# A graph attention layer with residual and layer norm: the last blocks put in another order, and a branch's transfers on another queue

## The chip, the cores and the metric

The kernel runs on one core of one Trainium2 chip. The core has five engines that run their own instruction streams: TensorE (PE; its weight loads are shown as PEld), VectorE (DVE), ScalarE (ACT), GpSimd (POOL) and SyncE (SP), which here only issues transfers. Sixteen DMA engines move data between the memory (HBM) and the on-chip memory (SBUF); TensorE writes to PSUM, which VectorE and ScalarE read and GpSimd doesn't. The metric is the device time of one execution in microseconds, as the median of several runs.

## What is computed

```python
def _L0_gnn_ref(h, adj_mat, W, a):          # 4 heads, 512 hidden
    ht = (h @ W).reshape(N, 4, 512).transpose(1, 0, 2)
    src = einsum('hnd,hd->hn', ht, a[:, :512, 0])
    dst = einsum('hnd,hd->hn', ht, a[:, 512:, 0])
    e = leaky_relu(src[:, :, None] + dst[:, None, :], 0.01) + adj_mat[None]
    att = softmax(e, axis=-1)
    return einsum('hij,hjd->hid', att, ht).mean(axis=0)

x = layernorm(x + _L0_gnn_ref(x, adj, W, a), axis=-1)      # eps 1e-5
```

`x` is 4096 x 512 and `adj` 4096 x 4096, both float32 (64 MB of `adj`). The entries of `adj` go up to 1e9 and are added to the scores before the softmax. Where the largest entry of a row leads the second largest by more than the scores can differ, the softmax is 1 at that column and 0 elsewhere, and the row's attention is one row of `x` times the mean of the four heads' `W`.

## The kernel before

`leading_rows` assumes that every row has such a leader, computes the output from it, and then tests whether it was true. `general` computes the whole layer the long way; it stands behind a branch (lines 61 to 63) on the number of rows that fail. With these inputs no row fails and the branch isn't entered. Its instructions are still part of the program, and at the place where the two ways meet each engine brings its semaphores to the values that they would have after the branch.

There are NB = 32 blocks of 128 rows. A loop over t = 0 to 31 is a software pipeline that is written out by hand; the order in the text is the order on each engine. For a block `ib`:

- `load_adj` (L118, SyncE) loads 2 MB of `adj`, five blocks ahead; the last four blocks come in two or four pieces. `load_x` (L121) loads rows of `x` into `hold`, which keeps all 32 blocks and becomes the output.
- `segment_maxima` (L163, VectorE) takes the maximum of each 32 columns; `find_segment` (L168 to L182) finds the segment of the largest one (`at`), and on GpSimd computes its address (`row`), fetches these 32 numbers with an indirect DMA (`lead`) and computes `start`.
- two steps later `find_column` takes the second largest in the segment (`find_inner`), finds the position, computes the column on GpSimd (`col`, L200), and `gather_rows` fetches that row of `x` as `y` (L186, indirect DMA). The last block uses `find_column_in_row` instead: VectorE searches the whole row of 4096 (L206).
- `turn` (L213, L215): four transposes on TensorE, and a copy to SBUF on ScalarE (`yt`). `products` (L228): four products with the mean of the heads' weights, summed in PSUM (`o`). `residual` (L221) adds the block's `x` to the same sum by a product with the identity; `residual_in_halves` (L266) does so for the last block, whose product is made in two halves (L270).
- blocks 0 to 23: `stats` (two ScalarE passes), `rstd` (GpSimd) and `finish` (ScalarE, L261) normalise. `row_norm` (L235) sums the squares of `x` for the test.

BEHIND = 24 and LATE = 28. Blocks 24 to 27 get their `x` late: `put_by` parks the products in SBUF and `add_x` (L244) adds `x` afterwards. Blocks 27 to 31 use `moments` (bn_stats on VectorE, square root on ScalarE, L287), `factor` (L290, L292) and `normalise` (VectorE, L297).

What follows the loop (L463 to L525) is the tail, again in hand-written order: the stores of blocks 0 to 23 (L313), the rest of blocks 24 to 31, the bound and test (`bound`, `test`, `count`, `report`) and the last six stores. All loads and stores of this part are issued by SyncE, in order, on eight semaphores in turn; a transfer waits until the one eight places ahead of it has landed. A store that isn't ready holds up those behind it. GpSimd issues its gathers itself.

In `general` the transfers are issued by GpSimd (L555, L557, L592, L632, L643).

Of the kernel before, what the change touches and what calls it, by code (L numbers as in the profile page):

```python
# [20 lines left out]
P = 128  # L21
# [45 lines left out]
def leading_rows(ctx, tc, x, adj, W, a, out, ident, v, n_bad, any_bad):  # L67
# [100 lines left out]
    def find_segment(ib):  # L168
        seg = seg_of.pop(ib)
        nc.vector.max(out=top[:, ib, :], in_=seg)  # L170
        at = small.tile([P, 8], U32, name="at")
        nc.vector.max_index(at, top[:, ib, :], seg)  # L172
        row = small.tile([P, 1], U32, name="row")
        nc.gpsimd.tensor_tensor(row, at[:, 0:1], first[:, ib : ib + 1], op=OP.add)  # L174
        lead = lead_pool.tile([P, E], F32, name="lead")
        nc.gpsimd.indirect_dma_start(  # L176
            out=lead, out_offset=None, in_=adj_segs,
            in_offset=bass.IndirectOffsetOnAxis(ap=row[:, :1], axis=0),
        )
        start = at_of[ib] = small.tile([P, 1], U32, name="start")  # L180
        nc.gpsimd.tensor_tensor(start, at[:, 0:1], width, op=OP.mult)  # L181
        lead_of[ib] = lead  # L182

    def gather_rows(ib, col):
        y = y_t[ib] = y_pool.tile([P, D], F32, name="y")
# [73 lines left out]
    def finish(ib):  # L259
        i = slice(ib, ib + 1)  # L260
        nc.scalar.activation(hold[:, ib, :], o_ps.pop(ib), AF.Identity, bias=nm[:, i], scale=sd[:, i])  # L261

    def residual_in_halves(ib):
        o_ps[ib] = [psum.tile([P, D // 2], F32, name="o") for _ in range(2)]
        for k, o in enumerate(o_ps[ib]):
            nc.tensor.matmul(o, ident, hold[:, ib, ts(k, D // 2)], start=True, stop=False)  # L266
# [22 lines left out]
    def factor(ib, shift=False):  # L289
        nc.vector.reciprocal(rt[ib], rt[ib])  # L290
        if shift:
            nc.vector.scalar_tensor_tensor(  # L292
                nm[:, ib : ib + 1], mean_var[ib][:, 0:1], -1.0, rt[ib], op0=OP.mult, op1=OP.mult
            )

    def normalise(ib, o, columns=slice(0, D)):
# [107 lines left out]
    vectors = [(kb, h) for kb in range(KB) for h in range(H)]  # L404
    vectors_at = {t: 2 if t < 3 else 1 for t in range(1, 15)}
    COLUMN, PROJECT, STATS, FINISH = 2, 3, 4, 6

    for t in range(NB):
        if t == NB // 2:
            tc.mark_branch_hint_location("general", engines=HINTED)  # L410
        if t in x_at:
            load_x(*x_at[t])
        if t + AHEAD == NB - 1:
            load_x(LATE, Q)
        load_adj(t + AHEAD)
# [12 lines left out]
        if t < 2:  # L428
            mean_of_heads(t)
        elif t == 2:  # L430
            mean_of_heads(2)
            mean_of_heads(3)
        if t == 0:
            turn_a()
        turned = [(*vectors[0], turn_w(*vectors.pop(0))) for _ in range(vectors_at.get(t, 0))]
        if t == 16:
            head_norms()
        ib = t - PROJECT
        if t == NB - 1:
            for late in range(LATE, NB):  # L440
                row_norm(late)
            residual(LATE)
            residual(LATE + 1)
        if ib >= 0:
            turn(ib)
            if ib > BEHIND:
                products(ib - 1, KB - 1, KB)
            if ib < BEHIND:
                residual(ib)
        for some in turned:  # L450
            head_vector(*some)
        if ib >= 0:
            products(ib, 0, KB if ib < BEHIND else KB - 1)
        if t >= BEHIND + STATS:
            put_by(t - STATS)
        elif t >= STATS:
            stats(t - STATS)
            row_norm(t - STATS)
        if pair:
            finish(t - FINISH)  # L460
            finish(t - FINISH + 1)

    for ib in range(BEHIND, LATE):  # L463
        row_norm(ib)
    for ib in range(0, 2 * Q, Q):
        store(nc.sync, ib, Q)
    for ib in range(2 * Q, BEHIND, 2):
        store(nc.sync, ib, 2)
    find_column(NB - 2)
    add_x(nc.gpsimd, BEHIND)  # L470
    add_x(nc.gpsimd, BEHIND + 1)
    find_column_in_row(NB - 1)
    add_x(nc.gpsimd, BEHIND + 2)
    products(LATE, KB - 1, KB)
    residual_in_halves(NB - 1)
    turn(NB - 3)
    products(NB - 3, 0, KB - 1)
    moments(LATE)
    for ib in range(BEHIND, NB):
        find_inner(ib)  # L480
    bound(0)
    products(NB - 3, KB - 1, KB)
    stats(BEHIND)
    factor(LATE)
    normalise(LATE, o_ps.pop(LATE))
    bound(1)
    turn(NB - 2)
    bound(2)
    add_x(nc.vector, LATE - 1)
    stats(BEHIND + 1)  # L490
    moments(LATE - 1)
    products(NB - 2, 0, 2)
    bound(3)
    test()
    pg = count()
    products(NB - 2, 2, KB - 1)
    stats(BEHIND + 2)
    rstd(slice(BEHIND, BEHIND + 2))
    rstd(slice(BEHIND + 2, BEHIND + 3))
    moments(NB - 3)  # L500
    report(pg)
    turn(NB - 1)
    factor(LATE - 1, shift=True)
    factor(NB - 3)
    normalise(NB - 3, o_ps.pop(NB - 3))
    finish(BEHIND)
    finish(BEHIND + 1)
    products(NB - 2, KB - 1, KB)
    products_of_half(NB - 1, 0)
    products_of_half(NB - 1, 1)  # L510
    nc.vector.tensor_add(hold[:, NB - 2, :], o_ps[NB - 2], hold[:, NB - 2, :])
    o_ps[NB - 2] = hold[:, NB - 2, :]
    moments(NB - 2)
    stats_of_half(NB - 1, 0)
    factor(NB - 2)
    normalise(NB - 2, o_ps.pop(NB - 2))
    finish(BEHIND + 2)
    finish(BEHIND + 3)
    stats_of_half(NB - 1, 1)
    moments(NB - 1)  # L520
    factor(NB - 1, shift=True)
    finish_in_halves(NB - 1)
    for ib, n in ((NB - 4, 1), (NB - 3, 1), (BEHIND, 2), (NB - 2, 1), (BEHIND + 2, 2)):
        store(nc.sync, ib, n)
    store(nc.sync, NB - 1, 1)  # L525

# [2 lines left out]
def general(ctx, tc, x, adj, W, out, ident, v, n_bad):  # L529
# [20 lines left out]
    with ExitStack() as pre:  # L550
# [1 line left out]
        two = pre.enter_context(tc.tile_pool(name="two", bufs=2))  # L552
        pps = pre.enter_context(tc.tile_pool(name="pps", bufs=2, space=bass.MemoryType.PSUM))
        for g in range(NCH):
            nc.gpsimd.dma_start(x_sb[:, ts(g, Q), :], x_blocks[:, ts(g, Q), :])  # L555
        for kb in range(KB):
            nc.gpsimd.dma_start(w_sb[:, kb, :], w_blocks[:, kb, :])  # L557
        for g in range(NCH):
            xT = two.tile([P, KB, C], F32, name="xT")
            for q in range(Q):  # L560
# [26 lines left out]
    def block(ib):  # L587
# [1 line left out]
        nc.vector.tensor_copy(src_i, src[:, ds(ib, 1), :].rearrange("p o h -> p (o h)"))  # L589
        held = psum.tile([P, D], F32, name="o_ps", bufs=1)  # L590
        adj_t = score.tile([P, N], F32, name="adj_g")
        nc.gpsimd.dma_start(adj_t, adj[ds(ib, P, NB), :])  # L592
        for h in range(H):
            s = score.tile([P, N], F32, name="s")
            nc.scalar.activation(s, dst_b[:, h, :], AF.Identity, bias=src_i[:, h : h + 1])
# [33 lines left out]
                    start=(h == 0 and kb == 0), stop=(h == H - 1 and kb == KB - 1),  # L629
                )  # L630
        r = turned.tile([P, D], F32, name="y_g")
        nc.gpsimd.dma_start(r, x[ds(ib, P, NB), :])  # L632
        nc.vector.tensor_add(r, r, held)
        st = stat.tile([P, nc.vector.BN_STATS_DIM], F32, name="st_g")
        nc.vector.bn_stats(st, r)
# [4 lines left out]
        nc.scalar.activation(sd, sd, AF.Sqrt)  # L640
        nc.vector.reciprocal(sd, sd)
        nc.vector.tensor_scalar(r, r, mv[:, 0:1], sd, op0=OP.subtract, op1=OP.mult)
        nc.gpsimd.dma_start(out[ds(ib, P, NB), :], r)  # L643

    with tc.For_i(0, NB, 1) as ib:
        of_block = stat.tile([1, 1], I32, name="of_block", bufs=1)
# [32 lines left out]
```

## Time and profile before

| | us |
|---|---|
| runs: median, lowest, highest (3 runs) | 235.95, 235.95, 236.46 |
| the profiled execution | 236.21 |
| its span | 234.6 |
| VectorE busy / TensorE busy | 188.4 / 195.2 |
| ScalarE busy / GpSimd busy | 111.6 / 101.2 |
| moved by the DMA engines | 97.21 MB, 414 GB/s over the span |

Times inside the profile count from the start of its span. The page gives the busy share of each engine in 40 equal slices, the chain of work that ended last, and groups of instructions with their mean duration. Other answers of the trace list instructions in order of time, what an engine waited for, and busy times by stretches. A wait is put down to what ended last before it. The first groups of the page are these (line, engine, operation, output and inputs, shapes, count, busy us and mean ns, idle us before and what ended it):

```profile
L163 DVE TENSOR_REDUCE seg<-adj_t 128x64 f32<-128x2048 f32 (+1 forms) x68 | 146.0, 2149 | 32.7 <-DMA adj_t<-in_adj_dram 32.3
L228 PE MATMUL o<-w_sum,yt 128*128 128x512 f32 x248 | 115.1, 605 | 1.7 <-ACT yt L215 1.7
```

A product counts as two matmuls there, and its 605 ns overlap with the next one: TensorE takes a new product every 0.86 us.

### The profile page before, as it was taken

How to read it: one execution, taken by the hardware profiler on the slowest of the kernel's cores; microseconds unless marked ns; L12 is line 12 of the kernel's file. 1: busy time of each engine (PE TensorE's matmuls, PEld its weight loads, DVE VectorE, ACT ScalarE, POOL GpSimd, SP SyncE). 2: the span in 40 equal slices, each digit the busy share in tenths (PEclk: the TensorE clock that was granted, in tenths of full speed). 3: DMA queues.
4: the chain of work that ended last, by engine and by line, in shares of the span. 5: the costliest groups of instructions: out<-in, count | busy, mean ns of one | idle time of the engine just before them, and what ended most of it. 6: DMA issues, size and time to landing. Idle time of an engine off the chain costs nothing.

```text
span 234.6 us, 2498 instructions
## 1 busy us (share of the span) xinstructions
PE 195.2 (83%) x683; PEld 101.4 (43%) x683; DVE 188.4 (80%) x302; ACT 111.6 (48%) x267; POOL 101.2 (43%) x215
## 2 busy tenths in 40 slices
PE   0188929999999999999979879797998968698990
PEld 0034514756565655555534333242443423244460
DVE  1736875589869995999589989998799999989672
ACT  2012011255474747474758354646464645166582
POOL 1012232414527462646353645464365464549130
PEclk9999977999999999999999999999799999999998
DMA  6999999999999999999999999999999999999985
GB/s 226 439 428 426 443 425 430 415 440 412 440 420 426 424 437 434 425 424 428 427 432 433 425 433 422 432 418 429 425 432 418 422 425 427 411 425 419 417 355 210
DMA packets 13697, 97.21 MB, mean 414 GB/s; under 512 B 2152, under 2 KB 2664, under 8 KB 7792
## 3 DMA queue, kind: packets, MB, share of 16 engines
q1 hardware_dynamic: 10080, 88.08, 88.9%
q0 software_dynamic: 3584, 8.92, 9.6%
q8 instruction: 6, 0.10, 0.2%
q14 instruction: 11, 0.09, 0.1%
q10 hardware_dynamic: 16, 0.02, 0.0%
HBM read 88.62 MB, written 8.39 MB: 414 GB/s over the span
## 4 chain that ended last, share of the span: by engine, by line
DMA 45%; POOL 17%; issue 15%; PE 10%; DVE 9%; ACT 1%; POOLq 0%; SPq 0%; DVEq 0%
DMA adj_t<-in_adj_dram 42%; DVE seg L163 8%; PE o L228 7%; POOL lead L176 6%; POOL y L186 5%; DMA y<-in_x_dram,col 3%; POOL sd L256 2%; PE o L270 2%; POOL start L181 1%; POOL row L174 1%; POOL col L200 1%; PE tp L213 1%; PE o L221 1%; ACT yt L215 1%; POOL sd L255 1%
## 5 line engine op out<-in xcount | busy, mean ns | idle before, releaser
L163 DVE TENSOR_REDUCE seg<-adj_t 128x64 f32<-128x2048 f32 (+1 forms) x68 | 146.0, 2149 | 32.7 <-DMA adj_t<-in_adj_dram 32.3
L228 PE MATMUL o<-w_sum,yt 128*128 128x512 f32 x248 | 115.1, 605 | 1.7 <-ACT yt L215 1.7
L228 PEld LDWEIGHTS o<-w_sum,yt 128*128 128x128 f32 x248 | 44.5, 191 | 54.8 <-issue 42.3
L215 ACT COPY yt<-tp 128x512 f32<-128x512 f32 x32 | 18.8, 588 | 44.3 <-PE tp L213 44.3
L176 POOL DMA_INDIRECT lead<-in_adj_dram,row x32 | 32.3, 1010 | 15.5 <-POOL row L174 15.0
L186 POOL DMA_INDIRECT y<-in_x_dram,col x32 | 30.9, 965 | 15.4 <-POOL col L200 15.2
L318 PE MATMUL o<-hold,ident 128*128 128x512 f32 x32 | 18.9, 745 | 17.5 <-DMA hold<-in_L_gnn_W_dram 17.5
L213 PE MATMUL tp<-ident,y 128*128 128x128 f32 x128 | 20.0, 280 | 12.6 <-DMA y<-in_x_dram,col 12.6
L221 PE MATMUL o<-hold,ident 128*128 128x512 f32 x52 | 27.3, 611 | 0.0
L213 PEld LDWEIGHTS tp<-ident,y 128*128 128x128 f32 x128 | 14.9, 143 | 25.4 <-issue 25.0
L174 POOL TENSOR_TENSOR row<-at,first 128x1 uint32<-128x1 uint32 x32 | 6.1, 190 | 42.0 <-DVE at L172 42.0
L336 ACT COPY wt<-tp 128x512 f32<-128x512 f32 x16 | 9.2, 587 | 31.4 <-PE tp L334 31.4
L200 POOL TENSOR_TENSOR col<-start,within 128x1 uint32<-128x1 uint32 x31 | 5.9, 190 | 40.1 <-DVE within L198 40.1
L235 ACT ACTIVATE sq<-hold 128x512 f32<-128x512 f32 x32 | 19.8, 619 | 0.0
L342 PEld LDWEIGHTS pv<-at_d,wt 128*128 128x128 f32 x128 | 16.3, 191 | 6.8 <-ACT wt L336 4.0
L318 PEld LDWEIGHTS o<-hold,ident 128*128 128x128 f32 x32 | 7.4, 243 | 26.7 <-POOL row L174 11.0
L319 ACT ACTIVATE w_sum<-o 128x512 f32<-128x512 f32 x4 | 2.4, 598 | 33.9 <-PE o L318 33.9
L261 ACT ACTIVATE hold<-o,nm,sd 128x512 f32<-128x512 f32 x24 | 17.2, 771 | 0.0
L252 ACT ACTIVATE sq<-o,nm 128x512 f32<-128x512 f32 x24 | 16.5, 688 | 0.8
L342 PE MATMUL pv<-at_d,wt 128*128 128x2 f32 x128 | 15.3, 244 | 0.6 <-ACT wt L336 0.6
L250 ACT ACTIVATE sq<-o 128x512 f32<-128x512 f32 x24 | 14.6, 609 | 0.0
L334 PEld LDWEIGHTS tp<-ident,hold 128*128 128x128 f32 x64 | 7.9, 142 | 6.9 <-issue 6.9
(85 smaller groups left out, 139.8 us busy)
## 6 DMA issues: line engine op xcount, KB each, us to landing
adj_t<-in_adj_dram SPq DMA_DIRECT2D x27, 2048.0 KB, 31.3
hold<-in_x_dram SPq DMA_DIRECT2D x7, 1024.0 KB, 33.2
adj_t<-in_adj_dram SPq DMA_DIRECT2D x6, 1024.0 KB, 25.7
out_dram<-hold SPq DMA_DIRECT2D x10, 512.0 KB, 15.2
adj_t<-in_adj_dram SPq DMA_DIRECT2D x8, 512.0 KB
hold<-in_L_gnn_W_dram SPq DMA_DIRECT2D x4, 1024.0 KB
out_dram<-hold SPq DMA_DIRECT2D x2, 1024.0 KB
hold<-in_x_dram SPq DMA_DIRECT2D x2, 512.0 KB, 14.1
```

The source lines that it names most:

```text
L163: nc.vector.tensor_reduce(seg_of[ib][:, ts(k, S // n)], adj_t[ib][:, ts(k, N // n)].rearrange("p (s e) -> p s e", e=E), axis=AX.X, op=OP.max,)
L176: nc.gpsimd.indirect_dma_start(out=lead, out_offset=None, in_=adj_segs, in_offset=bass.IndirectOffsetOnAxis(ap=row[:, :1], axis=0),)
L186: nc.gpsimd.indirect_dma_start(out=y, out_offset=None, in_=x, in_offset=bass.IndirectOffsetOnAxis(ap=col[:, :1], axis=0),)
L213: nc.tensor.transpose(tp[:, kb, :], y[:, ts(kb, P)], ident)
L215: nc.scalar.copy(yt, tp)
L221: nc.tensor.matmul(o_ps[ib], ident, hold[:, ib, :], start=start, stop=False)
L228: nc.tensor.matmul(o_ps[ib], yt_of[ib][:, kb, :], w_sum[:, kb, :], start=(start and kb == 0), stop=(kb == KB - 1),)
L235: nc.scalar.activation(sq, hold[:, ib, :], AF.Square, accum_out=xx[:, ib : ib + 1])
L252: nc.scalar.activation(sq, o, AF.Square, bias=nm[:, i], accum_out=sd[:, i])
L261: nc.scalar.activation(hold[:, ib, :], o_ps.pop(ib), AF.Identity, bias=nm[:, i], scale=sd[:, i])
L318: nc.tensor.matmul(o, ident, hold[:, w_at + kb * H + h, :], start=(h == 0), stop=(h == H - 1))
L342: nc.tensor.matmul(pv[:, kb, h : 2 * H : H], wt[:, k, :], at_d[:, k, h : 2 * H : H], start=(k == 0), stop=(k == KB - 1),)
```

## The change

Five things are changed.

1. The transfers of `general` are issued by SyncE instead of GpSimd.
2. `find_segment` is split: its GpSimd part is now `fetch_segment`, which follows at once for all blocks but the last. For block 31 it comes in the tail, behind the gather of block 30 and the add of block 24, and without `start`, which isn't used there.
3. The residual of block 29 leaves TensorE: `add_residual` adds it on VectorE when the product is done, as was done for block 30. The halves' residual of block 31, the turns of 29 and 30 and the last products of 28 and 29 change places. The add of block 27 goes from VectorE to GpSimd.
4. Blocks 24 to 26 are finished on GpSimd (`finish_on_chip`) and block 27 on ScalarE earlier than before. The test's count and report come later.
5. The stores of blocks 0 to 23 and of 24 to 30 are issued in another order, in the same sizes. `factor` uses another VectorE operation for the same product.

```diff
     def find_segment(ib):
...
+        if ib < NB - 1:
+            fetch_segment(ib)
+
+    def fetch_segment(ib):
+        at = at_of.pop(ib)
         row = small.tile([P, 1], U32, name="row")
...
         lead_of[ib] = lead
+        if ib < NB - 1:
+            start = at_of[ib] = small.tile([P, 1], U32, name="start")
+            nc.gpsimd.tensor_tensor(start, at[:, 0:1], width, op=OP.mult)
...
+    def finish_on_chip(ib):
+        i, h = slice(ib, ib + 1), hold[:, ib, :]
+        o_ps.pop(ib)
+        nc.gpsimd.tensor_scalar(h, h, sd[:, i], nm[:, i], op0=OP.mult, op1=OP.add)
+
+    def add_residual(ib):
+        nc.vector.tensor_add(hold[:, ib, :], o_ps[ib], hold[:, ib, :])
+        o_ps[ib] = hold[:, ib, :]
...
-            nc.vector.scalar_tensor_tensor(
-                nm[:, ib : ib + 1], mean_var[ib][:, 0:1], -1.0, rt[ib], op0=OP.mult, op1=OP.mult
+            nc.vector.tensor_scalar(
+                nm[:, ib : ib + 1], mean_var[ib][:, 0:1], rt[ib], -1.0, op0=OP.mult, op1=OP.mult
             )
...
+    HELD = ((8, 2), (10, 2), (0, Q), (12, 2), (14, 2), (Q, Q), (16, 2), (18, 2), (20, 2), (22, 2))
...
             residual(LATE)
-            residual(LATE + 1)
...
-    for ib in range(0, 2 * Q, Q):
-        store(nc.sync, ib, Q)
-    for ib in range(2 * Q, BEHIND, 2):
-        store(nc.sync, ib, 2)
+    for ib, n in HELD:
+        store(nc.sync, ib, n)
     find_column(NB - 2)
     add_x(nc.gpsimd, BEHIND)
-    add_x(nc.gpsimd, BEHIND + 1)
+    fetch_segment(NB - 1)
     find_column_in_row(NB - 1)
-    add_x(nc.gpsimd, BEHIND + 2)
+    for ib in (BEHIND + 1, LATE - 1, BEHIND + 2):
+        add_x(nc.gpsimd, ib)
+    turn(NB - 3)
     products(LATE, KB - 1, KB)
+    products(NB - 3, 0, KB - 1)
+    stats(BEHIND)
+    moments(LATE)
+    bound(0)
     residual_in_halves(NB - 1)
-    turn(NB - 3)
-    products(NB - 3, 0, KB - 1)
-    moments(LATE)
-    for ib in range(BEHIND, NB):
+    for ib in range(BEHIND, NB - 1):
         find_inner(ib)
-    bound(0)
-    products(NB - 3, KB - 1, KB)
-    stats(BEHIND)
+    bound(1)
     factor(LATE)
     normalise(LATE, o_ps.pop(LATE))
-    bound(1)
     turn(NB - 2)
+    products(NB - 3, KB - 1, KB)
     bound(2)
-    add_x(nc.vector, LATE - 1)
     stats(BEHIND + 1)
     moments(LATE - 1)
-    products(NB - 2, 0, 2)
+    find_inner(NB - 1)
     bound(3)
     test()
-    pg = count()
-    products(NB - 2, 2, KB - 1)
+    products(NB - 2, 0, KB - 1)
     stats(BEHIND + 2)
     rstd(slice(BEHIND, BEHIND + 2))
+    finish_on_chip(BEHIND)
+    finish_on_chip(BEHIND + 1)
     rstd(slice(BEHIND + 2, BEHIND + 3))
+    finish_on_chip(BEHIND + 2)
+    add_residual(NB - 3)
+    turn(NB - 1)
     moments(NB - 3)
-    report(pg)
-    turn(NB - 1)
     factor(LATE - 1, shift=True)
+    finish(LATE - 1)
     factor(NB - 3)
     normalise(NB - 3, o_ps.pop(NB - 3))
-    finish(BEHIND)
-    finish(BEHIND + 1)
     products(NB - 2, KB - 1, KB)
     products_of_half(NB - 1, 0)
+    pg = count()
     products_of_half(NB - 1, 1)
-    nc.vector.tensor_add(hold[:, NB - 2, :], o_ps[NB - 2], hold[:, NB - 2, :])
-    o_ps[NB - 2] = hold[:, NB - 2, :]
+    add_residual(NB - 2)
     moments(NB - 2)
     stats_of_half(NB - 1, 0)
     factor(NB - 2)
     normalise(NB - 2, o_ps.pop(NB - 2))
-    finish(BEHIND + 2)
-    finish(BEHIND + 3)
+    report(pg)
     stats_of_half(NB - 1, 1)
     moments(NB - 1)
     factor(NB - 1, shift=True)
     finish_in_halves(NB - 1)
-    for ib, n in ((NB - 4, 1), (NB - 3, 1), (BEHIND, 2), (NB - 2, 1), (BEHIND + 2, 2)):
+    for ib, n in ((LATE, 1), (BEHIND, 2), (NB - 3, 1), (BEHIND + 2, 2), (NB - 2, 1)):
         store(nc.sync, ib, n)
     store(nc.sync, NB - 1, 1)
...
-            nc.gpsimd.dma_start(x_sb[:, ts(g, Q), :], x_blocks[:, ts(g, Q), :])
+            nc.sync.dma_start(x_sb[:, ts(g, Q), :], x_blocks[:, ts(g, Q), :])
...
-            nc.gpsimd.dma_start(w_sb[:, kb, :], w_blocks[:, kb, :])
+            nc.sync.dma_start(w_sb[:, kb, :], w_blocks[:, kb, :])
...
-        nc.gpsimd.dma_start(adj_t, adj[ds(ib, P, NB), :])
+        nc.sync.dma_start(adj_t, adj[ds(ib, P, NB), :])
...
-        nc.gpsimd.dma_start(r, x[ds(ib, P, NB), :])
+        nc.sync.dma_start(r, x[ds(ib, P, NB), :])
...
-        nc.gpsimd.dma_start(out[ds(ib, P, NB), :], r)
+        nc.sync.dma_start(out[ds(ib, P, NB), :], r)
```

More of the change, by code (lines that the diff above doesn't have):

```diff
@@ L170, in find_segment @@
         nc.vector.max(out=top[:, ib, :], in_=seg)
-        at = small.tile([P, 8], U32, name="at")
+        at = at_of[ib] = small.tile([P, 8], U32, name="at")
         nc.vector.max_index(at, top[:, ib, :], seg)
+        if ib < NB - 1:
+            fetch_segment(ib)
+    def fetch_segment(ib):
+        at = at_of.pop(ib)
         row = small.tile([P, 1], U32, name="row")
@@ L179, in find_segment @@
         )
-        start = at_of[ib] = small.tile([P, 1], U32, name="start")
-        nc.gpsimd.tensor_tensor(start, at[:, 0:1], width, op=OP.mult)
         lead_of[ib] = lead
+        if ib < NB - 1:
+            start = at_of[ib] = small.tile([P, 1], U32, name="start")
+            nc.gpsimd.tensor_tensor(start, at[:, 0:1], width, op=OP.mult)
     def gather_rows(ib, col):
```

## The prediction

> **What bounds the kernel now.** I read the page first (span, slices, chain), then the busy time by stretches of the tail, then the chain of waits from 203 us on, and at last the instructions of the lines that open and close the program.
>
> ```profile
> span 234.6 us, 2498 instructions
> ...
> PE   0188929999999999999979879797998968698990
> DMA  6999999999999999999999999999999999999985
> GB/s 226 439 428 426 443 425 430 415 440 412 440 420 426 424 437 434 425 424 428 427 432 433 425 433 422 432 418 429 425 432 418 422 425 427 411 425 419 417 355 210
> ```
>
> Up to slice 38 the DMA engines are full: 97.21 MB at some 425 GB/s. The change moves the same bytes, so all that it can win lies at the start, in the last 10 us, and in what comes after the last store.
>
> ```profile
> 220.00:225.00 5.00, 4.63 (x20) 2.42 (x19) 4.04 (x20) 3.95 (x12) 1.67 (x5) 1.00 1.03 415
> 225.00:230.00 5.00, 4.23 (x18) 2.96 (x16) 3.74 (x9) 3.60 (x7) 0.37 (x2) 1.00 0.78 304
> 230.00:234.60 4.60, 0.00 (x0) 0.00 (x0) 0.78 (x3) 0.83 (x2) 0.00 (x0) 0.84 0.49 192
> ```
>
> These are stretch, length, busy us of PE, PEld, DVE, ACT and POOL, clock, DMA share, GB/s: from 225 us the DMA has holes, because the last stores are not ready. What they wait for is in the chain of waits (start, us, what):
>
> ```profile
> 207.78 1.72 PE o L221 x4
> 209.49 0.44 PE tp L213 x4
> ...
> 214.31 0.86 PE o L266 x4
> 215.17 0.45 PE tp L213 x4
> ...
> 215.64 0.59 ACT yt L215
> ...
> 220.57 0.59 ACT yt L215
> ...
> 225.69 3.55 PE o L270 x16
> ...
> 229.27 0.44 DVE halves_st L304
> ...
> 230.69 0.56 ACT hold L310
> ```
>
> TensorE is the chain from 203.58 to 229.24, with two holes of 0.6 us while ScalarE copies a turned block. Two residuals stand in it (1.72), and the halves' residual of block 31 (0.86) comes where there is no hole. From the last product to the end of ACT L310 it takes 2.01 us; the last store is issued at 231.29 and its semaphore is full at 233.60 (2.31). The program's own end and start, by line (ns shortest/median/longest, first and last start):
>
> ```profile
> L62 POOLq INC_SWDGE_SEM  x1: 1476/1476/1476, 226.7 to 226.7; - x1
> ```
> ```profile
> L674 SPq EVENT_SEMAPHORE  x14: 17/28/28, 232.8 to 234.5; - x14
> ...
> L674 POOLq DRAIN  x3: 40/103/5306, 228.2 to 234.3; - x3
> ```
> ```profile
> L665 POOLq MOVE  x4: 29/29/35, 0.2 to 0.4; - x4
> ```
>
> GpSimd balances its DMA semaphores in the branch not taken (L62, 1.48 us) and then drains for 5.31 us, from 228.23 to 233.54, 0.2 us before SyncE reaches the closing barrier at 233.74. So GpSimd's end is nearly the bound today and would be, were it to get there later. SyncE's twelve closing waits run from 232.83 at 0.064 us each, so that all but the last are over when the store lands.
>
> **What the skill says.** "GPSIMD Engine Reference", 3.1, gives 769 ns measured for a one-input loop over 512 elements and about twice VectorE's time for two inputs; the trace has 1.28 us for the two-input add (L244) against 0.67 us on VectorE, which agrees, and no one-input GpSimd operation of this size. "VectorE: DVE Perf Modes", Why PSUM operands drop a tier, says that a PSUM source loses the faster mode: L297 takes 0.81 us from PSUM and 0.55 from SBUF here. "DMA: Bandwidth & Descriptors", Anatomy of one DMA, puts a fixed cost near 2 us on a transfer, mostly the receipt of the last byte; the last store's 2.31 us for 256 KB agrees.
>
> **The change, part by part.**
>
> Start. The four GpSimd MOVEs at 0.21 to 0.42 us belong to the general path's transfers and go to SyncE, which now waits for GpSimd at the opening barrier. GpSimd's memsets and drain move up 4 x 0.06 = 0.24 us, and the first load with them: -0.24 (bounds 0 to -0.3).
>
> TensorE. From 207.78: one residual 0.86, turn 0.44, last product of 27 0.86, three of 28 2.57, so 212.6. The turn of 29 now comes before the last product of 28, and its gather (issued 206.05) lands at 212.90 by the trace's semaphores: start 213.05. Turn, last of 28, three of 29 end at 216.9: the copy of 29 hides behind 28's product. Transpose of the bound 0.11, halves' residual 0.86: 217.9. The gather of 30 is issued behind `col` alone, at 211.2 instead of 212.00; with its 6.45 us it lands at 217.6, so there is no wait. Turn 0.44, last of 29 0.86, 0.11, three of 30 2.57: 222.0. The gather of 31 stands behind one add instead of two, but behind the moved lead fetch: issue 215.1 instead of 215.65 (VectorE's index ends at 214.84), 7.09 us, landed 222.2. Turn 222.35, product, two halves of 1.78, count 0.11: end 227.4 instead of 229.24.
>
> VectorE. It loses the add of 27 and gets the add of block 29's residual (0.72, paid for by L297 from SBUF, 0.57 for 0.81); the test comes earlier than it is needed. Block 29's root waits on ScalarE behind the copy of 31 (223.6), so normalising 29 ends at 224.7. Then, on VectorE alone: add 0.72, statistics 0.82, half statistics 0.43, reciprocal 0.18, normalise 0.57, report 0.50, in all 3.2: it reaches the last half's statistics at 228.0, not at TensorE's 227.5. Before: 229.27. Gain 1.3; without the report, which earlier stood at 223.4, it would be 1.7. The range is 0.9 (gather latencies of 7.3 and 7.5) to 1.7 (6.4 both).
>
> ScalarE loses three finishes (0.72 each) and is not late. GpSimd: adds of 25, 27, 26 end at 220.0, roots of 24 and 25 1.3, two finishes, root of 26 1.1, one finish. One finish on GpSimd is not in the trace. Bounds: 0.44 us (512 elements at the page's port bound of 1.03 cycles at 1.2 GHz, an estimate) and 2.7 us (twice the two-input row). I take 0.8 (the page's 769 ns): done at 225.6; at 1.25 it is 227.0. The store of 26 and 27 waits for that one, and behind it on SyncE stand the stores of 30 and 31; at up to 2 us it is in time.
>
> Landing. With 1.3 + 0.24, the last store is issued at 229.75 and could land at 232.05. But one of the sixteen DMA engines lags: the store of 28 has fifteen parts by 227.42 and the last at 228.46, and from there this engine has nearly no pause. Its own times are 0.6 us for 256 KB (230.81 to 231.41) and 1.21 for 512 KB (to 232.62). From 228.46 - 0.24: 1.2 + 0.6 + 1.2 + 0.6 + 0.6 gives 232.4 for the last store. Bounds: 232.05 without the lag (231.75 if the latency falls to 2.0, as for its other parts), 233.0 if the 0.55 that the store of 24 and 25 took beyond 1.21 (1.76, an instruction fetch beside it) comes again. I take 232.4: -1.2 against 233.60.
>
> Close. The general path's transfers on SyncE make it balance its eight hardware DMA semaphores in the branch not taken, each a wait for all earlier transfers. The last of these waits for the last store; only then come a branch and the twelve closing waits. Before, the landing was followed by the drain after 0.09 us; now by 0.09 + 0.03 + 12 x 0.064 = 0.88: +0.79 (bounds 0.6 and 1.0). This is new on the path. GpSimd's 1.48 + 5.31 us go; that wins nothing itself (0.2 us of slack), but without it the finishes and the late report, which ends near 228, would have cost about 3 us. Behind the closing waits nothing else is queued.
>
> The new order of the held stores moves no bytes and no start of the queue (199 us); eight stay in flight, at least 4 MB, some 9 us of work: 0, with bounds of 0.2 either way. `factor` with the other operation: 0.16 us either way.
>
> Sum: -1.2 (start included) + 0.79 = -0.4. The profiled execution is 236.21 with 1.6 us around its span, so 235.8; the median of the runs is 235.95, so 235.5.
>
> **Rivals.**
> A, the landing follows the compute: no lagging engine, latency 2.0 to 2.3: -1.55 to -1.85 + 0.79 = about -1.0, 234.9. For it: DMA share 0.78 after 225, so fifteen engines do have room. Against: the sixteenth.
> B, the slower one: GpSimd's finishes. With price p the last ends at 223.2 + 3p, and the last store is issued 0.75 later and lands 2.3 after that, all less 0.24. It is slower than before from p = 2.3 (landing above 232.8); at 2.7 it is +1.3, 237.2. For it: GpSimd is the slow elementwise engine and the scalars are per-partition pointers. Against: one input, where the two-input add takes 1.28.
> C, the gathers give nothing: y of 31 right behind the lead fetch lands where it did or 0.5 later; TensorE ends near 228.3, VectorE is 0.4 to 0.9 earlier, and the closing waits eat it: about 236.0, no change.
>
> **How the numbers follow.** 0.3% (0.7 us) is about what can be told from no change. Forecast, 0.48: 235.5 (own range 235.1 to 236.2). A 0.32, B 0.13, C 0.07. Faster: most of A and a little of the forecast's edge, 0.34. Slower: B and a lag with the dearest close, 0.15. Same: 0.51. For eight in ten the range takes in A and the cheap end of B: 234.7 to 236.8.
>
> **What would show it.** Right: the first load near 0.75 us; TensorE's last product near 227.2; the last half's statistics near 227.8; SyncE's closing waits all after the landing, some 0.8 us of them; no long GpSimd drain. Wrong: a GpSimd finish over 2 us, a turn of 29 to 31 waiting over 1 us for its gather, the long drain still there, or a landing that is as late as before.

## The result, and the profile after

| | before | after |
|---|---|---|
| median of 12 runs each | 236.04 | 237.93 |
| lowest, highest | 235.63, 236.46 | 236.91, 240.34 |
| profiled execution, its span | 236.21, 234.6 | 237.32, 235.5 |
| last store issued, landed, span's end | 231.29, 233.60, 234.56 | 230.48, 233.79, 235.55 |

The changed kernel is slower: ratio 1.0093, 95% interval 1.0071 to 1.0115. Ratios, here and below, are not quotients of the medians (1.0080 here), and leave out executions that lie over 1.5% above their kernel's fastest, of which the table of experiments has five (two of `after_early`, two of `after_early_hint`, one of `idle_finishes`). The times of the changed kernel also spread over 3.4 us, those of the kernel before over 0.8 in these twelve runs; larger sets further down spread more.

The busy times by stretches of the changed kernel (columns as before: stretch, length, PE, PEld, DVE, ACT, POOL, clock, DMA share, GB/s):

```profile
220.00:225.00 5.00, 5.00 (x18) 2.69 (x18) 3.57 (x16) 4.26 (x12) 3.14 (x7) 1.00 1.01 411
225.00:230.00 5.00, 3.36 (x16) 2.31 (x15) 4.21 (x15) 0.84 (x4) 1.21 (x3) 1.00 0.97 385
230.00:235.50 5.50, 0.00 (x0) 0.00 (x0) 0.30 (x1) 0.45 (x1) 0.00 (x0) 0.56 0.21 77
```

The DMA holes from 225 to 230 us are gone (0.97 for 0.78): the tail does deliver its blocks earlier. What is left is 5.5 us in which only 0.4 MB move, 256 KB of it the last store. The chain of waits at its end (start, us, what):

```profile
226.44 1.94 PE o L285 x8
...
228.40 0.44 DVE halves_st L319
...
229.89 0.56 ACT hold L325
```

It is 0.81 us earlier than before (230.45 for 231.26), of which 0.24 come from the start. The transfers of `out`, from issue to landing, are first those of before, then of after (shortest, median, longest); the shortest is the last store:

```profile
DMA to landing us min/median/max: 2.3/8.8/15.2
```
```profile
DMA to landing us min/median/max: 3.3/9.6/15.3
```

Fourteen of the last store's sixteen parts land within 1.99 us, two at 3.31. So the store that is issued 0.81 us earlier lands 0.19 later. Last, the program's own end in the changed kernel, by line:

```profile
L62 SPq EVENT_SEMAPHORE  x9: 17/17/17, 232.2 to 233.8; - x9
```
```profile
L687 SPq EVENT_SEMAPHORE  x14: 17/28/28, 233.9 to 235.5; - x14
L687 POOLq EVENT_SEMAPHORE  x4: 17/17/17, 234.8 to 235.4; - x4
L687 POOLq DRAIN  x3: 40/103/5306, 229.4 to 235.3; - x3
```

SyncE's balancing in the branch (L62) lasts until the landing, and all its closing waits come after it: from landing to the span's end it takes 1.76 us, before 0.96. GpSimd's drain of 5306 ns is still there. It starts at 229.42, since the report of the test is ready only at 228.23 (before: 223.83), and ends at 234.73, level with SyncE (last drain at 234.67). The balance of the two profiled executions in span: -0.81 (issue) + 1.00 (landing) + 0.80 (close) = +0.99.

### The profile page after: what moved, and what is told of

It is laid out like the page before. It is cut to its first block, busy times and chain, and to the rows that moved or that the text cites. A ratio compares the mean times of both kernels' runs of the same rounds, so it can differ in the third digit from the quotient of the medians.

```text
span 235.5 us, 2496 instructions
## 1 busy us (share of the span) xinstructions
PE 196.5 (83%) x681; PEld 101.1 (43%) x681; DVE 188.0 (80%) x302; ACT 109.7 (47%) x264; POOL 104.6 (44%) x218
## 4 chain that ended last, share of the span: by engine, by line
DMA 45%; POOL 19%; issue 19%; DVE 9%; PE 4%; ACT 0%; POOLq 0%; SPq 0%; DVEq 0%
DMA adj_t<-in_adj_dram 42%; DVE seg L163 8%; POOL lead L181 6%; POOL y L192 6%; DMA y<-in_x_dram,col 3%; PE o L234 2%; POOL sd L262 2%; PE o L285 2%; POOL start L188 1%; POOL row L179 1%; POOL col L206 1%; POOL sd L261 1%; DVE at L172 0%; PE tp L219 0%; DVE top L170 0%
## 5 line engine op out<-in xcount | busy, mean ns | idle before, releaser
L333 PE MATMUL o<-hold,ident 128*128 128x512 f32 x32 | 18.9, 746 | 14.9 <-DMA hold<-in_L_gnn_W_dram 14.9
L227 PE MATMUL o<-hold,ident 128*128 128x512 f32 x50 | 26.6, 614 | 0.3 <-DMA hold<-in_x_dram 0.3
```

The lines of the kernel that those rows point to most:

```text
L227: nc.tensor.matmul(o_ps[ib], ident, hold[:, ib, :], start=start, stop=False)
L333: nc.tensor.matmul(o, ident, hold[:, w_at + kb * H + h, :], start=(h == 0), stop=(h == H - 1))
```

## The experiments

All times are in us; a ratio is to the runs of before on the same chip in the same set. Theory D is GpSimd's drain, S is SyncE's longer close. The lowest time is shown because the medians of several kernels hold disturbances that the lowest don't.

| run | n | lowest | median | highest | ratio, interval |
|---|---|---|---|---|---|
| before_late | 5 | 239.03 | 239.20 | 240.08 | 1.0139, 1.0106 to 1.0172 |
| after_pool | 4 | 239.24 | 239.32 | 239.43 | 1.0132, 1.0096 to 1.0167 |
| before_sync | 22 | 236.30 | 236.77 | 238.81 | 1.0034, 1.0018 to 1.0050 |
| before_sync_hint | 17 | 236.65 | 237.18 | 238.66 | 1.0050, 1.0028 to 1.0072 |
| after_early | 11 | 236.63 | 238.52 | 240.90 | 1.0091, 1.0055 to 1.0128 |
| after_early_hint | 18 | 236.78 | 237.16 | 240.67 | 1.0059, 1.0037 to 1.0082 |
| after_early_pool | 17 | 235.97 | 237.94 | 239.41 | 1.0064, 1.0035 to 1.0094 |
| early_pool_again | 4 | 236.15 | 237.17 | 238.07 | 1.0019, 0.9993 to 1.0045 |
| after_act_finish | 14 | 235.30 | 235.73 | 237.46 | 0.9996, 0.9974 to 1.0018 |
| act_finish_again | 22 | 235.35 | 236.10 | 238.59 | 0.9990, 0.9967 to 1.0013 |
| after_early_actf | 22 | 236.10 | 236.86 | 239.37 | 1.0034, 1.0011 to 1.0056 |
| idle_finishes | 13 | 236.58 | 237.59 | 240.20 | 1.0070, 1.0044 to 1.0097 |
| late_branch | 5 | 240.20 | 240.79 | 241.56 | 1.0197, 1.0173 to 1.0221 |
| before_again | 14 | 235.57 | 236.13 | 238.74 | 1.0005, 0.9979 to 1.0031 |
| after_again | 6 | 237.41 | 238.90 | 240.51 | 1.0103, 1.0060 to 1.0146 |
| act_finish_behind | 6 | 236.34 | 238.27 | 239.80 | 1.0095, 1.0063 to 1.0127 |
| after_warm | 22 | 237.40 | 237.91 | 238.64 | 1.0065, 1.0049 to 1.0082 |
| behind_warm | 14 | 236.29 | 236.71 | 238.13 | 1.0015, 0.9992 to 1.0037 |

### GpSimd's drain: the late count alone, and the general path moved back

`before_late` is the kernel before with the test's count and report where the change has them; `after_pool` is the changed kernel with the transfers of `general` on GpSimd.

```diff
-    pg = count()                        # before_late
     products(NB - 2, 2, KB - 1)
...
     products_of_half(NB - 1, 0)
+    pg = count()
...
-        nc.sync.dma_start(adj_t, ...)   # after_pool, and four more
+        nc.gpsimd.dma_start(adj_t, ...)
```

> The kernel before with only the count and the report moved back to where the changed kernel has them (report after normalising block 30). Theory D: any_bad is known near 229.1 instead of 223.8, then load, branch, semaphores and balancing 2.9 us, the drain ends near 237.3: 3.6 us slower, 239.6. Theory S: SyncE reads any_bad only after the last store is issued, so nothing changes: 236.0 to 236.4.

> The changed kernel with the general path's transfers back on GpSimd. Theory D: GpSimd gets its semaphore waits (0.45 us) and the balancing (1.48) back in front of the drain, which then ends near 236.65: 1.9 us slower than the changed kernel, about 239.5. Theory S: the balancing by SyncE goes, so 1 to 2 us faster than the changed kernel, 235.5 to 236.5.

Both are slower than before by 3.3 and 3.5 us (medians), as theory D had it; the times are narrow, in five and four runs. GpSimd's and SyncE's drains of `before_late`, by line:

```profile
L674 POOLq DRAIN  x3: 40/103/5306, 231.3 to 237.2; - x3
L674 SPq DRAIN  x3: 7/7/7, 234.1 to 236.9; - x3
```

and of `after_pool`:

```profile
L687 POOLq DRAIN  x3: 40/103/5306, 231.7 to 237.6; - x3
L687 SPq DRAIN  x3: 7/7/7, 234.4 to 237.3; - x3
```

SyncE is ready at 234.1 and 234.5 and waits until GpSimd's long drain is over, at 236.65 and 237.05. The drain is 5306 ns in all twenty profiles, with and without the DMA semaphores to balance (INC_SWDGE_SEM, 1.48 us): it belongs to the end of the program, and it starts when GpSimd has learnt the test's result and has done its own work. In `before_late` it starts 3.1 us later than before (231.35 for 228.23). So the late count is dear, and the move of the transfers to SyncE is what makes it bearable: it takes 2.3 us out ahead of the drain (229.42 for 231.74 in `after_pool`), the 1.48 and the waits beside it, and not the drain itself.

### SyncE's close

`before_sync` is the kernel before with only the transfers of `general` on SyncE. In `after_early` the changed kernel counts and reports early again (after block 30's three products, and behind the finish of 27); `after_early_pool` has the transfers on GpSimd besides.

> The kernel before with only the general path's transfers moved to SyncE. Theory D: GpSimd's drain ends near 231.7, two us earlier, and isn't the bound, so D alone says no loss and 0.2 us won at the start: 235.8. Theory S: twelve closing waits and more come after the landing: +0.55 us at least, 236.6, and if SyncE's branch misses its instructions up to 238 with a wide spread.

> The changed kernel with count and report moved forward: the count's product right after the three products of block 30, the report on VectorE in its pause at 223.6 us. Theory D (GpSimd's drain of 5.31 us is fixed, and starts only when GpSimd knows any_bad and has done its own work): the drain starts near 227.1 instead of 229.42 and ends near 232.4; if D alone is the loss, the time comes back to 236.0 to 236.3. Theory S (SyncE's close: eight semaphores balanced after the last landing, and its longer branch): no gain, since SyncE reached its end at 234.67 against GpSimd's 234.73: 237.3 to 237.9.

> The changed kernel with two parts undone: the count and report early again (after block 30's three products and behind the finish of 27), and the general path's transfers on GpSimd. Theory D+S (both GpSimd's drain and SyncE's longer close cost time): GpSimd's last finish ends near 225.8, its branch follows near 226.3, the drain comes 2.4 us later as in the run with only the general path moved back (229.31 to 231.74), so it runs from 228.7 to 234.0; SyncE's close is again one wait, 0.15 us after the last store's landing (233.3 at the latest). Span 233.9 to 234.2, time 235.5 to 235.8, and all times within 1 us. Theory D alone (SyncE's close is innocent, the spread of the early-count run comes from the remade tail itself): times spread from 236.6 to 241 again, median over 237.5.

In `before_sync` GpSimd's drain ends at 231.13, out of the way, and yet the lowest time rises by 0.8 (236.30 for 235.49 in that set). Its close, by line:

```profile
L62 SPq EVENT_SEMAPHORE  x9: 17/17/17, 232.5 to 233.1; - x9
```
```profile
L674 SPq EVENT_SEMAPHORE  x14: 17/28/28, 233.1 to 234.7; - x14
```

Landing at 233.04, then twelve closing waits. In the pairs that differ in this alone, the lowest time differs by 0.66 (`after_early` and `after_early_pool`) and 0.80 (`after_early_actf` and `after_act_finish`); the second pair ran in two sets whose lowest times of the kernel before are 0.15 apart, which leaves 0.65. Some 0.2 of it lie outside the span: a run is 1.73 to 1.94 us longer than its span with these transfers on SyncE, 1.50 to 1.71 otherwise.

A second guess was that SyncE's branch is to blame: it takes 0.50 us to its next event where it took 0.18. The Trainium skill ("Runtime: NRT & Kernel Launch", Instruction fetch mechanics) says that a branch out of the window already fetched stalls for a fetch, and the trace does show one more fetch of 8 KB. The four other engines have a branch hint; SyncE got one too:

```diff
-HINTED = ... ("PE", "Activation", "DVE", "Pool")
+HINTED = ... ("PE", "Activation", "DVE", "Pool", "SP")
```

> The kernel before with only the general path's transfers on SyncE (236.77, 236.3 to 238.8 without a hint), and SyncE hinted. If the unhinted branch makes the 0.9 us: 235.9 to 236.2, narrow. If the closing semaphores do: 236.6 to 237, as without.

> The early-count kernel with the general path's transfers on SyncE, and SyncE added to the engines that have a branch hint (the only edit). If SyncE's unhinted branch, with its fetch of instructions, makes the spread (238.5 median, 236.6 to 240.9): branch to next event back at 0.2 us, median near 236.0 to 236.5 and a narrow spread. If the eight semaphores balanced at the end, or the landing itself, make it: as without the hint, median over 237.5 with a spread over 3 us.

No: the branch still takes 0.52 us and the lowest times are 0.15 to 0.35 higher than without, in another set. The median of `after_early_hint` is lower than that of `after_early`, 237.16 for 238.52, while its highest time is as high (240.67 for 240.90); medians of kernels with such a spread depend on how many executions fall into it.

The early count has shown something else. `after_early` has its drain over at 231.63 and a lowest time only 0.3 below the changed kernel's, but a median above it. `after_early_pool`, with neither fault, ranges from 236.0 to 239.4. Theories D and S had no such spread; only the second branch of the last expectation, that the remade tail itself spreads the times, had it. That branch's other half, that SyncE's close is innocent, does not hold: the lowest time is 0.66 lower.

### What spreads the times: two wrong turns

In `after_act_finish` ScalarE finishes 24 to 26 again; `after_early_actf` has the same with the transfers on SyncE; `idle_finishes` gives GpSimd the three operations back, on other data and into a spare tile. `late_branch` puts two spare operations on ScalarE and VectorE ahead of their branches, in `after_early_pool`, which is also the run that the first expectation calls the run before.

```diff
-    finish_on_chip(BEHIND)          # after_act_finish
-    finish_on_chip(BEHIND + 1)
+    finish(BEHIND)
...
     finish(LATE - 1)
+    finish(BEHIND + 1)
+    finish(BEHIND + 2)
```

> As the run before, and 24 to 26 finished on ScalarE again (24 when its factors are ready, 25 and 26 behind 27), so that GpSimd's last work is the shift of 26 near 225. Theory D+S: GpSimd's drain from 227.3 to 232.6, off the path; what ends the span is the last store's landing (232.3 to 233.3) plus 0.15. Span 232.6 to 233.6, time 234.2 to 235.2, which is below the kernel before by about 1 us: the gain that the prediction gave the earlier products. If the earlier last store is worth nothing (theory L: the instruction fetches after the branches delay its last parts to 233.3 or later whatever the issue), 235.0 to 235.6. D alone: median over 237.

> The early-count kernel with the general path on SyncE (238.52, 236.6 to 240.9), and 24 to 26 finished on ScalarE. If moving the finishes is what took the spread away in the run on GpSimd, it does here too: median 236.2 to 236.8, which is 0.6 to 0.9 us over that run (SyncE's close). If the spread comes with SyncE's close: median over 237.5.

> The run with 24 to 26 finished on ScalarE (235.73, 235.3 to 237.5), with GpSimd given the same three operations at the same places, on other data and into a spare tile that nobody reads. GpSimd's end comes 0.9 us later, so its drain ends near 233.5, still in time. Theory F (GpSimd's late elementwise work beside the others makes the spread): median over 237, spread over 3 us. Theory L (it is where the branches and the last store fall): median 235.6 to 236.0, narrow.

> The run with the early count and the general path on GpSimd (237.94, 236.0 to 239.4), with two spare copies on ScalarE and two spare bn_stats on VectorE behind their last halves, so that both branch more than 1 us later, away from the last store. Theory L (the instruction fetches that follow these two branches collide with the last store's parts, and make the spread): the last parts of the last store land with the others, 2.3 us after its issue, and the times are narrow, median 235.4 to 235.8. Theory F (GpSimd's late finishes make the spread): nothing changes, median 237 to 238.5, spread over 3 us.

> The early-count kernel with the general path on GpSimd once more, for a second profile of it: with a time over 237.5 the trace shows where a disturbed execution loses its 1.5 to 3 us. Theory L: at the last store, whose last parts land 3 us or more after its issue. Theory F: before it, in GpSimd's finishes or in VectorE's work beside them. Theory G: the gathers of 30 or 31 land later than 7.8 us after their issue, and the turns wait.

`after_act_finish` is as fast as the kernel before, and its profile has the shortest span of all, 234.05. The gain of 1 us that was expected isn't there: the gather of 29 takes 7.68 us, its turn waits 2.16 for it, and the last store is issued 0.5 earlier than before. Nor did moving the finishes take the spread away: in 22 runs `after_early_actf` ranges over 3.3 us, and `act_finish_again`, the same kernel as `after_act_finish`, over 3.2. `idle_finishes` seemed to convict GpSimd's finishes, but its drain ended at 234.85 instead of the 233.5 that I had expected, which about accounts for the 1.3 us of its lowest time; what makes its highest times isn't shown. `late_branch` can't be read: its spare tiles moved the tiles behind them by 4120 bytes, and it loses 4.0 us before the tail (the gather of block 27 is issued at 200.26, in `after_early_pool` at 196.24). Why wasn't tried. Its last store has fifteen parts within 1.97 us and the last at 2.47.

The second profile of the same program, `early_pool_again`, is an execution of 238.07. SyncE's queue at its start is first that of `after_early_pool` (236.18), then its own (start, us, engine, line, operation):

```profile
7.08 0.33 SPq L124 DMA_DIRECT2D hold<-in_L_gnn_W_dram  x1
```
```profile
8.40 0.33 SPq L124 DMA_DIRECT2D hold<-in_L_gnn_W_dram  x1
```

This issue waits for an earlier load to land. It is 1.3 us late in the same program, because the first loads were slow, and 1.2 us of that are still there at the gather of block 27 (197.47 for 196.24). None of the three theories had this; the last store takes 3.28 us here and 3.41 in the faster execution. Such starts occur with other kernels too: this issue comes at 8.46 in `before_sync_hint` (237.89) and at 6.95 in `before_sync` (236.65). So they explain part of a spread, but not why the changed kernel has more of it.

### TensorE's pauses and its clock

The two programs as they are, and the version above with the finishes of 24 and 26 further back:

> The kernel before, as the kernel under test. If the spread belongs to the changed program: 235.9 median, 235.5 to 236.9 with a few above, ratio 1.000. If it belongs to the place in a round that the kernel under test has: median 236.5 to 237.5 with a spread of 3 us, and then the ratio of every kernel here holds such a part.

> The changed kernel once more. If the spread belongs to the program: lowest 236.9, median 237.7 to 238.3, up to 240. If it was an accident of the first set of runs: median 237.2, most within 0.6 us.

> The version with 24 to 26 finished on ScalarE again, beside the one above on the same chip: lowest 235.2 to 235.4, median 235.6 to 235.9.

> The version with the early count, the general path on GpSimd and 24 to 26 finished on ScalarE, with the finish of 24 moved behind block 31's turned copy and that of 26 behind block 30's square root. In the version before it the finish of 24 held that copy up by 0.6 us (224.31 against 223.62). If the last store's landing ends the span, the last product ends 0.6 us earlier (228.0 instead of 228.7), the last store lands near 232.5 and the lowest time is 234.6 to 234.9, the median near 235.0 to 235.4 (before: 235.5 and 236.0). If the landing does not follow the issue (the last parts late, as in the other kernels with an earlier issue): lowest 235.2 to 235.5.

Both kernels spread, and the changed one more often: 8 of its 18 runs lie more than 1.5 us above the lowest of their set, and 25 of the 216 runs of the kernel before that stand in all sets together. `act_finish_again` came out 0.2 above its expected median, and `act_finish_behind` missed both its branches (236.34 at the lowest, median 238.27). And `after_again` was profiled in an execution of 240.36. TensorE there, in order of time (in brackets the pause before, and what ended it):

```profile
208.72 3.68 PE L234 MATMUL o<-w_sum,yt 128*128 128x512 f32 x8
215.01 0.63 PE L219 MATMUL tp<-ident,y 128*128 128x128 f32 x4 [2.61 <-DMA y<-in_x_dram,col]
215.48 5.29 PE L234 MATMUL o<-w_sum,yt 128*128 128x512 f32 x8
```

and in the first profile of the changed kernel:

```profile
212.36 0.63 PE L219 MATMUL tp<-ident,y 128*128 128x128 f32 x4 [0.84 <-DMA y<-in_x_dram,col]
212.83 3.68 PE L234 MATMUL o<-w_sum,yt 128*128 128x512 f32 x8
...
218.62 0.63 PE L219 MATMUL tp<-ident,y 128*128 128x128 f32 x4 [1.13 <-DMA y<-in_x_dram,col]
```

The same eight matmuls take 5.29 instead of 3.68 us. The busy times by stretches of `after_again` tell why (last three columns: granted clock, DMA share, GB/s):

```profile
215.00:216.00 1.00, 0.98 (x6) 0.67 (x6) 0.02 (x1) 0.32 (x1) 0.26 (x2) 1.00 1.05 430
216.00:217.00 1.00, 1.00 (x3) 0.61 (x2) 0.08 (x1) 0.97 (x4) 0.98 (x2) 0.50 1.02 418
...
218.00:219.00 1.00, 1.00 (x2) 0.34 (x1) 0.56 (x7) 0.16 (x1) 1.00 (x2) 0.50 1.00 414
219.00:220.00 1.00, 1.00 (x3) 0.47 (x2) 0.00 (x0) 0.00 (x0) 1.00 (x2) 0.79 0.95 393
```

From 216.00 to 219.41 the clock is 0.50. The last half's statistics start 2.94 us later than in the first profile. Of this, 0.90 were there before the tail (the gather of 29 is issued at 206.57, there at 205.67), and the half clock costs 1.61. The gather of 29 also takes 8.31 us instead of 6.55, of which 1.13 come back, since the wait for the gather of 30 falls away (the terms add up to 3.1).

The Trainium skill ("TensorE: Matmul & The Clock Gate", Part 1) describes free-running windows of 3413 ns and half the clock after an idle one. The trace agrees on the length: every stretch of clock ahead of the program's end is 3.413 us or a multiple of it. But the window ahead of 216.00 was not idle: TensorE paused for 2.42 of its 3.41 us. A pause of which 2.0 us fell in one window (2.89 in all, in `after_early_actf`) was let pass. So it depends on where a pause falls among the windows, and that differs from one execution to the next: measured from the start of the span, their edges lie 1.05 us apart in the two profiles of the changed kernel.

The twenty traces together give the share. From 50 us to the last stretch of clock they hold 1041 such windows, and in each I added up the time in which no matmul ran. Where it was 2.03 us or more, the next window had half the clock in 24 cases of 24; from 1.80 to 2.00 in 3 of 12; below that in 2 of 1005, both times the window itself had half the clock already. Most of these lie where the DMA engines are full and TensorE is not the limit, in the kernel before too (at 164.84 us). The one at 216.00 in `after_again` is the only one in any of the tails after 204 us.

In the kernel before, TensorE's longest pause after 204 us is 0.68, in `before_again` 0.91; in the changed kernel and its relatives it is 1.1 to 2.9, each time for a gather, of 28, 29 or 30.

Half the clock isn't the whole spread. Each run also has its mean clock on record, and some high ones leave no room for a window of half clock in the tail: the changed kernel's 238.54 has 0.988, 238.90 in `after_early` 0.990, 237.94 and 238.35 in `after_early_pool` 0.988. That is 4.7 to 5.7 us of half clock in all (twice the missing share of the span), where every profile has at least 3.4 at its start and 1.2 at its end. The runs of 239 us and more have 10 us or more of it in all kernels but two that are slow throughout (`before_late` and `late_branch`), so there is room for such a window in these.

The test fills these pauses with work that nobody needs, in the changed kernel (`after_warm`) and in `act_finish_behind` (`behind_warm`):

```diff
         tp = psum.tile([P, KB, P], F32, name="tp", bufs=2)
+        for _ in range(6 if LATE <= ib < NB - 1 else 0):
+            nc.tensor.transpose(tp[:, 0, :], w_sum[:, 0, 0:P], ident)
         for kb in range(KB):
```

> The changed kernel with six spare 128x128 transposes (some 0.9 us of TensorE) ahead of the turns of 28, 29 and 30, which wait for nothing and write what the turn overwrites. Theory T (a pause of TensorE for a gather gets the next 3.4 us half the clock in some executions, and that is the spread): the pauses fall under 1.7 us, no window of 0.50 between 205 and 230 us, most times within 0.8 us, median 237.2 to 237.8, at most one in five over 238.5. If the pauses are not the cause: 237 to 240.5 again, median 237.9 to 238.9, or 0.5 more by the spare work.

> The version with the early count, the general path on GpSimd and 24 to 26 finished on ScalarE behind the copies (238.27, 236.3 to 239.8), with the same spare transposes. Theory T: median 235.2 to 236.0, most within 0.8 us, lowest 234.8 to 235.4, at or below the kernel before. If the pauses are not the cause: 236.3 to 240 again, median over 237.

TensorE of `after_warm` at the turns of 28 and 29:

```profile
207.20 0.82 PE L219 MATMUL tp<-ident,w_sum 128*128 128x128 f32 x6
208.78 0.66 PE L221 MATMUL tp<-ident,y 128*128 128x128 f32 x4 [0.76 <-DMA y<-in_x_dram,col]
209.28 3.68 PE L236 MATMUL o<-w_sum,yt 128*128 128x512 f32 x8
212.79 0.82 PE L219 MATMUL tp<-ident,w_sum 128*128 128x128 f32 x6
213.45 0.60 PE L221 MATMUL tp<-ident,y 128*128 128x128 f32 x4
```

The longest pause is 0.76, the clock is 1.00 from 38.52 to 233.08, and the spread is gone: 22 runs within 1.24 us, 2 of them over 238.5, where 8 of 18 runs of the changed kernel were. The changed kernel itself wasn't run in this set, but the kernel before spreads there over 4.1 us (235.59 to 239.69). The median stays at 237.91, 0.1 above what I expected, because the lowest time rises by 0.5: the spare work costs where the gather was early. The same work at a place where it fills no pause was not tried. `behind_warm` tightens likewise, to 1.8 us in 14 runs, but missed its expected 235.2 to 236.0 and isn't faster than before; its last product isn't earlier than in `after_act_finish`, and its last store lands 3.26 us after its issue. No version here is shown to beat the kernel before; `after_act_finish` equals it.

### The two late parts of the last store

No run isolates these; the twenty profiles do line up. VectorE's and ScalarE's branches are followed by fetches of instructions, 8 KB each. Where the first fetch after VectorE's and ScalarE's branches comes less than 1.5 us after the last store's issue (ten profiles, 0.97 to 1.49), the store takes 3.03 to 3.41 us; at 1.56 or more (seven, the kernel before among them) 2.15 to 2.47; at 1.50 to 1.54 both occur (2.19, 2.33, 3.44). That the fetch delays the store's parts on one or two DMA engines fits, and is not shown.

## Why the prediction was wrong

**Landing, the step that failed.** The prediction gave -1.2 for the last store, start included, which is a landing at 232.4; it was +0.19 in the profile, 233.79. Its lagging DMA engine behaved as reckoned up to there: the last parts of the five stores ahead landed at 228.22, 229.47, 230.09, 231.38 and 231.96, where its steps give 228.2, 229.4, 230.0, 231.2 and 231.8, and its last step of 0.6 would have ended at 232.6. What it did not have is that two of the sixteen parts of the last store took 3.31 us from the issue, where 2.65 were reckoned and 2.31 were needed before; even the prediction's bound with a fetch of instructions beside the store, 233.0, is passed by 0.8. With 2.31 the store would have landed at 232.79. So 1.0 to 1.2 of the 1.4 us that the landing is late belong to these two parts; what delays them stays open.

**Compute.** The rest is here: the last half's statistics were to start at 228.0 less 0.24, and started at 228.40. The step said of the gather of 30 that it "lands at 217.6, so there is no wait", with the latency that block 30 had before (6.45). It took 7.76 and landed at 218.48; TensorE waited 1.13 us for it, and 0.84 for that of 29. In the twenty profiles the gathers of 27 to 31 take 5.9 to 8.5 us. Rival C reckoned with gathers that give nothing: its end of TensorE near 228.3 and its gain of 0.4 to 0.9 on VectorE came about (228.36 and 0.87), though by the gather of 30 and not that of 31.

**The clock, which no step has.** The new order left TensorE with pauses that the old one didn't have, and a pause that fills more than 2 us of a window was followed by half the clock for 3.4 us. The prediction counted a late gather as its own wait. The median lies 0.6 above the profiled 237.32; filling the pauses took the times over 238.7 away. How much of the 0.6 is the clock isn't shown.

**Close.** +0.79 was predicted and +0.80 measured in the profile. Missing is what lies outside the span, some 0.2.

**GpSimd's drain.** "GpSimd's 1.48 + 5.31 us go" is wrong: 1.48 go, and some 0.8 of waits and a later branch with them, and 5.31 stay. In the changed kernel this costs nearly nothing, since drain and SyncE's close end together; it leaves no slack for anything later on GpSimd.

**Right.** The first load is issued at 0.74 (0.98 before), with the four MOVEs now on SyncE:

```profile
L678 SPq MOVE  x4: 29/34/42, 0.0 to 0.2; - x4
```

SyncE's closing waits all come after the landing, as forecast. And GpSimd's finish has the price that was taken, 0.8, so rival B's mechanism falls; the skill's 769 ns ("GPSIMD Engine Reference", 3.1) agrees with these:

```profile
L272 POOL TENSOR_SCALAR hold<-hold,sd,nm x3: 767/772/774, 222.8 to 225.6; 128x512 f32<-128x512 f32 x3
```

The last finish ended at 226.40 instead of 225.6. The terms that the prediction lists for GpSimd add up to 224.8, not to its 225.6, and GpSimd's wait from the last add (219.78) to the first root (221.42) isn't among them. This cost nothing: the store behind it was ready only at 227.9.

Of the four signs of being wrong that the prediction names, three came true: a turn that waits over 1 us, the long drain, and a landing as late as before.

## What to carry to other kernels

A tail that is shortened until it waits for transfers has to be costed with the slowest latency that these show, not with the one that the block had before, and TensorE's pauses in it can have a second price: half the clock for a whole window, in a part of the executions, which one profile need not show. An instruction that tells an engine that it may end (here the test's result for GpSimd) belongs early, ahead of work that can be late. And where a median rises more than the profiled execution does, one profile is not enough: the half clock here stood only in the trace of a high execution.

## What the runs showed of the hardware beyond this

GpSimd ended this program with a drain of 5306 ns in every kernel, whatever its work before. A window of 3.41 us in which TensorE paused for 2.03 us or more in all was followed by one of half clock each time (24 of 24), at 1.80 to 2.00 us in 3 of 12 cases. Transfers on SyncE in a branch that is never taken cost 0.65 to 0.8 us, some 0.2 of it outside the span.
